# Residual, values' bias and convolution's bias added by accumulating DMAs from GpSimd's queue instead of GpSimd additions, in a graph attention and convolution kernel

## The chip, the cores and the metric

One core of one Trainium2 chip. The metric is the device time in microseconds; lower is better. The program has five engines with queues of their own: TensorE (PE in the profile, its weight loads PEld), VectorE (DVE), ScalarE (ACT), GpSimd (POOL) and SyncE (SP), which here only issues DMAs. Sixteen DMA engines move data for all queues.

## The reference, cut to what matters

There are 32 items of 512 rows and 512 columns and one 512x512 adjacency matrix of zeros and ones. Each item goes through an attention layer (8 heads of 64) and a graph convolution, each with a residual and a layer norm. All is float32.

```python
q = (x @ Wq + bq).reshape(b, n, H, HD)          # k and v likewise
scores = jnp.einsum('bihd,bjhd->bhij', q, k) / jnp.sqrt(jnp.float32(HD))
scores = scores + jnp.where(adj == 0, -1e9, 0.0)
weights = jax.nn.softmax(scores, axis=-1)
att = jnp.einsum('bhij,bjhd->bihd', weights, v)
x = _layernorm(x + att)
norm_adj = adj * deg_inv_sqrt[:, None] * deg_inv_sqrt[None, :]
out = jnp.einsum('nm,bmo->bno', norm_adj, x @ weight) + bias
x = _layernorm(x + out)
```

Three additions in it are touched here: `x + att`, the bias `bv` of the values, and the convolution's `bias`.

## The kernel before, in words

The main path is `unshifted`, lines 50 to 961. A second program, `general`, runs only if a count of unfit numbers is above zero. The 32 items are taken in turn by the loop at line 843. An item `b` has two halves. Each half is a **stretch** of attention for two of the four groups of two heads (line 514: `sc`, the scores, then `av`, the products with the values), followed by a stretch of other matrix products. After the first stretch come the keys and queries of item `b + 1` (14 steps of `main`). After the second come the convolution of item `b - 1` (`conv["first"]`, then `conv["second"]`) and the values of item `b + 1`. Keys, values and convolution use seven products of sub-matrices instead of eight, and the values use the scheme twice.

The order is written out by hand. `play` (line 106) runs the steps of `main` and after step `n` what the table `beside` holds for `n`. Operations on TensorE, VectorE, ScalarE and GpSimd are issued through `InOrder`, so each engine's queue keeps program order, and the profile shows all of them at line 45. The DMAs on SP are not pinned; the framework sets their order and all semaphore waits. The tiles that matter:

- `YT[b]` (profile: `yT`), 128 partitions x 4 blocks of 512 columns, 1 MiB, two buffers: the attention's result, then the normed rows. VectorE transposes the product into `yb` and four DMAs scatter it into `YT` (line 509). `scale` (608) divides by the sums, on VectorE, in the item's own second half. `add` (615) adds the residual, on GpSimd, after step 0 of the *next* item's first half. Then `measure` (633), `root`, `norm` (643, ScalarE) and `low` (661, VectorE) follow in that half. `lift` (666) adds the convolution's bias, on GpSimd, after step 11. `grow` (670, ScalarE) scales `YT` in the second half, and the last additions of `convolve` read it.
- `R[b]` (profile: `xr`), 1 MiB: the rows of `x` for the residual, loaded by `load_residual` (184) with four SP DMAs of 256 KB, at line 848 near the start of the item after. It shares its space with `zT` of the convolution.
- `V[b]` (profile: `v`), 1 MiB, one buffer: the values. ScalarE puts and VectorE adds the products into it, and one GpSimd addition (`spread_last`, 401) lies between. `bias_values` (420) adds `bv_r`, a row copied to all 128 partitions, in four GpSimd additions. They are queued after step 17 of the second half, behind `combined` (the four subtractions `combine`, 165, on the turned `x` of item `b + 2`) and ahead of the accumulation of the exponentials (`acc`, line 466) of the next stretch.
- `wqv` (profile: `wqv`), 1792 KB of weights: it holds the queries' weights or the values' weights in turn. `swap` (259) fetches the other set with one SP DMA, for the values at the start of the second stretch, for the queries after step 17.

The attention's two loops and the table of the steady state's second half:

```python
for g in gs:
    scores(b, g)
for g in gs:
    accumulate(b, g)
...
beside = {
    1: parts[:1] + fold0, 3: parts[1:], 5: fold1, 6: grow[:1], 7: end["inverse"], 8: grow[1:2],
    9: grow[2:3] + scale[:1], 10: grow[3:] + scale[1:2], 11: scale[2:3], 13: turn0, 14: scale[3:],
    15: turn1 + combined[:2], 17: combined[2:] + back_to_queries + bias_v,
}
```

Of the kernel before, what the change touches and what calls it, by code (L numbers as in the profile page):

```python
# [15 lines left out]
ALU = mybir.AluOpType  # L16
AX = mybir.AxisListType

P = 128
# [31 lines left out]
def unshifted(  # L51
# [15 lines left out]
    B, N, D = x.shape  # L67
    NT = N // P
# [4 lines left out]
    LAST = B - 1  # L73
    tensor, vector, scalar, gpsimd = (InOrder(tc, e) for e in (nc.tensor, nc.vector, nc.scalar, nc.gpsimd))
# [17 lines left out]
    def bank(shape, name="mm"):  # L92
        psum["n"] += 1
        return psum["pool"].tile(shape, F32, name=name, tag=f"bank{-psum['n'] % 8}", bufs=1)
# [89 lines left out]
    def load_residual(b):  # L184
        if b < LAST - 1:
            t = acts.tile([P, NT, D], F32, name="xr", tag="zT", bufs=1)
        else:
            t = wk[:, 3:].rearrange("p k u o -> p k (u o)")
        R[b] = [t[:, i, :] for i in range(NT)]
        for i in range(NT):  # L190
            nc.sync.dma_start(R[b][i], x[b, ts(i, P), :])
# [174 lines left out]
    KQ, V = {}, {}  # L366
# [5 lines left out]
    def values_of(b):  # L372
# [44 lines left out]
        leaf = seven(LEAF, multiply_quarters, put_quarters, add_quarters, (4, P))  # L417
        return leaf + [spread_last] + seven(OUTER, multiply, put, add)

    def bias_values(b, n, engine=gpsimd):  # L420
        engine.tensor_add(V[b][:, n, :], V[b][:, n, :], bv_r)

# [27 lines left out]
    E, ACC, AV, SM, YT, HI, LO = {}, {}, {}, {}, {}, {}, {}  # L450
# [87 lines left out]
    def sums(b, c, p):  # L538
        for q in range(4):
            parts = ACC[b, ORDER[2 * c + q // 2]]  # L540
            for k, a in enumerate(parts):
                tensor.matmul(
                    p[32 * q : 32 * (q + 1), :], sel[:, c, :], a[:, q % 2, :],
                    start=k == 0, stop=k == len(parts) - 1,
                )
        if c == 0:
            SM[b] = wqv[:, 6].rearrange("p u n -> p (u n)")
            vector.tensor_scalar(SM[b], p, 1e-36, None, op0=ALU.max)
        else:
            vector.scalar_tensor_tensor(SM[b], p, 1e-36, SM[b], op0=ALU.max, op1=ALU.add)  # L550
# [23 lines left out]
    def finish(b):  # L574
# [16 lines left out]
        def inverse(c, p):  # L591
            sT = SM[b]
            p = p.rearrange("p (i a k r) -> p i a k r", i=NT, a=2, k=2)
            for i in range(NT):
                tensor.transpose(p[:, i].rearrange("p a k r -> p (a k r)"), sT[:, ts(i, P)], ident)
            if c == 0:
                t["inv"] = small.tile([P, NT, H], F32, name="inv")
            inv = t["inv"].rearrange("p i (a c k) -> p i a c k", a=2, c=2)
            vector.reciprocal(inv[:, :, :, c], p[:, :, :, :, c])
# [70 lines left out]
        def grow(i):  # L670
            x1 = YT[b][:, i, :]
            scalar.activation(x1, x1, AF.Copy, scale=rdeg[:, i : i + 1])

        all_, behind = range(NT), (NT - 1, *range(NT - 1))
        return dict(
            sums0=[lambda: sums(b, 0, bank([P, N]))], inverse0=[lambda: inverse(0, bank([P, N]))],
            sums1=[lambda: sums(b, 1, bank([P, N]))], inverse1=[lambda: inverse(1, bank([P, N]))],
            turn_values=[lambda: turn_values(ORDER[-1], bank([P, N]))],
# [5 lines left out]
            lift=each(lift, *((3, 0, 1, 2) if b == LAST else behind)),  # L684
            grow=each(grow, *(all_ if b == LAST else behind)),
# [128 lines left out]
    v = values_of(0)  # L814
# [28 lines left out]
    for b in range(B):  # L843
        one, two = ORDER[:2], ORDER[2:]
        f[b], c[b] = finish(b), convolve(b)
        ahead, back = f.get(b - 1), c.get(b - 2)
        if 1 < b < LAST:
            load_residual(b - 1)
        if b + 2 < B:
            load_x(b + 2, 0)  # L850
        if b == LAST:
            load_residual(b)
        stretch(b, one, back["measure"][:3] if back else ())

        def folds(gs):
            return [[lambda g=g, b=b: fold(b, g)] for g in gs]

        def turns(b=b + 2):
            if b >= B:
                return [], [], []  # L860
            return [lambda: turn(b, 0)], [lambda: turn(b, 1)], [lambda k=k: combine(b, k) for k in range(4)]

        fold0, fold1 = folds(one) if b < LAST else ([], [])
        rest = back["measure"][3:] + back["root"] if back else []
        store = back["store"] if back else []
        if b < LAST:
            k0, k1 = keys_and_queries(b + 1, 0), keys_and_queries(b + 1, 1)
            main = [p for pair in zip(k0, k1) for p in pair]
            if b == 0:
                exact = each(compare, *range(NT))  # L870
                weights = each(lambda k: weigh_part(w1, gpsimd, k), *range(4))
                beside = {
                    1: fold0, 2: [degrees], 3: weights[:1], 4: fold1, 5: weights[1:2] + exact[:1], 6: exact[1:2],
                    7: weights[2:3], 8: exact[2:3], 9: weights[3:], 10: exact[3:],
                }
            else:
                measure, norm, low = ahead["measure"], ahead["norm"], ahead["low"]
                scale = ahead["inverse"] + ahead["scale"] if b == 1 else []
                beside = {
                    0: rest + scale + ahead["add"], 1: store[:1] + fold0, 2: store[1:2], 3: store[2:3] + fold1,  # L880
                    4: store[3:] + measure[:2], 5: measure[2:] + ahead["root"] + [quarters], 7: norm[:1] + ahead["judge"],
                    8: norm[1:2] + low[:1], 9: norm[2:3] + low[1:2], 10: norm[3:] + low[2:3],
                    11: low[3:] + ahead["lift"],
                }
            play(main, beside)
        else:
            e = f[b]
            conv = c[b - 1]
            play(conv["first"], {
                0: rest + store[:1] + conv["parts"][:0], 1: store[1:2] + ahead["judge"] + conv["parts"][:1],  # L890
                2: store[2:] + e["sums0"],
                3: conv["parts"][1:] + e["inverse0"] + ahead["grow"],
            })

        if b < LAST:
            swap(1)
        stretch(b, two, f[b]["pairs"][0] + f[b]["pairs"][1] if b == LAST else ())

        fold0, fold1 = folds(two) if b < LAST else ([], [])
        turn0, turn1, combined = turns()  # L900
        if b + 2 < B:
            load_x(b + 2, 1)
        if b < LAST:
            end = f[b]
            v, bias_v = values_of(b + 1), each(bias_values, *((b + 1, n) for n in range(NT)))
            back_to_queries = [lambda: swap(0)] if b < LAST - 1 else []
            if b == 0:
                play(v, {
                    1: fold0, 5: fold1, 8: turn0, 9: turn1 + combined[:2], 10: bias_v + combined[2:] + back_to_queries,
                })  # L910
            else:
                conv = c[b - 1]
                second = conv["second"]
                k = 6 if b < LAST - 1 else 8
                main = conv["first"] + v[:k] + second[:1] + v[k:9] + second[1:2] + v[9:10] + second[2:3] + v[10:] + second[3:]
                grow, parts, scale = ahead["grow"], conv["parts"], end["scale"]
                if b < LAST - 1:
                    beside = {
                        1: parts[:1] + fold0, 3: parts[1:], 5: fold1, 6: grow[:1], 7: end["inverse"], 8: grow[1:2],
                        9: grow[2:3] + scale[:1], 10: grow[3:] + scale[1:2], 11: scale[2:3], 13: turn0, 14: scale[3:],  # L920
                        15: turn1 + combined[:2], 17: combined[2:] + back_to_queries + bias_v,
                    }
                else:
                    measure, norm, low = end["measure"], end["norm"], end["low"]
                    beside = {
                        0: [lambda: load_residual(LAST - 1)], 1: parts[:1] + fold0, 3: parts[1:], 5: fold1,
                        6: grow[:1], 7: end["inverse"], 8: grow[1:2] + scale[3:], 9: grow[2:3] + scale[:1], 10: grow[3:] + scale[1:3] + end["add"],
                        14: measure[:2], 15: measure[2:3], 16: measure[3:] + end["root"],
                        17: norm[:1] + bias_v, 18: norm[1:2] + low[:1], 19: norm[2:3] + low[1:2],
                        20: norm[3:] + low[2:3], 21: low[3:] + end["lift"],  # L930
                    }
                play(main, beside)
# [6 lines left out]
    end, held, e = f[LAST], c[LAST - 1], c[LAST]  # L939
# [17 lines left out]
    p = bank([1, 1])  # L957
# [287 lines left out]
```

## Time and profile before

| | |
|---|---|
| median of 3 runs | 2732.55 us (2730.91 to 2732.78) |
| the profiled execution, its own time | 2731.85 us |
| its span | 2730.0 us |
| TensorE's clock | 0.998 |
| busy: TensorE, VectorE, ScalarE, GpSimd | 2700.8, 2023.7, 1260.5, 2026.7 us |
| GpSimd: `acc` (374 additions of 128x1024) | 886.6 us |
| GpSimd: `v` + `bv_r`, `yT` + `b_r`, `yT` + `xr` | 160.6, 156.9, 149.2 us |
| DMA moved | 256.75 MB, mean 94 GB/s |
| `xr` loads on SP | 116 of 256 KB in the loop, median 3.5 us to landing |
| `wqv` swaps on SP | 61 of 1792 KB, median 7.6 and 7.0 us to landing |

A row of the timeline or of the groups names engine, line and operation, then the tile written, an arrow, and the tiles read. Times are from the start of the span. A value in square brackets is the idle time ahead of a row and what ended it. The chain of waits is followed back from the last instruction, at each step to what released it. In the windows, "DMA share" is the mean busy share of the sixteen DMA engines.

### The profile page before, as it was taken

Reading aid. Unit: us, or ns where it says so; the run is one execution under the profiler, and the core shown is the slowest. Engines: PE = TensorE matmul, PEld = TensorE weight load, DVE = VectorE, ACT = ScalarE, POOL = GpSimd, SP = SyncE. Lnnn points to the kernel's source line nnn. Section 1 sums busy time; section 2 is a strip of 40 time slices with the busy share of each in tenths; the row PEclk is TensorE's granted clock in tenths of the full one; section 3 lists DMA queues with packets and bytes.
Section 4 is the critical chain, followed back from the end, with each engine's and each line's share of the span. In section 5 each row is a group of like instructions: output and inputs, shape, how many; then the busy total and the mean of one; then the engine's idle time right before and its main releaser. Section 6 shows DMA issues by size and latency. Waiting matters only on the chain.

```text
span 2730.0 us, 36290 instructions
## 1 busy us (share of the span) xinstructions
PE 2700.8 (99%) x13284; PEld 1907.7 (70%) x13284; DVE 2023.7 (74%) x2809; ACT 1260.5 (46%) x1807; POOL 2026.7 (74%) x1335
## 2 busy tenths in 40 slices
PE   9999999999999999999999999999999999999997
PEld 6676676766767767767667677677676676766765
DVE  4777776777777778767777777777777776777777
ACT  3335444454444454444544445444445444454444
POOL 5778777778777787777777777877778777778775
PEclk9999999999999999999999999999999999999999
DMA  6222333323333233333232332333333333323321
GB/s 181 86 74 88 101 89 99 107 69 105 93 105 97 76 103 104 89 97 97 82 104 86 103 106 73 101 107 90 94 90 92 101 89 98 107 70 104 98 61 45
DMA packets 388186, 256.75 MB, mean 94 GB/s; under 512 B 278816, under 2 KB 346400, under 8 KB 379936
## 3 DMA queue, kind: packets, MB, share of 16 engines
q1 hardware_dynamic: 386848, 252.78, 30.8%
q8 instruction: 107, 1.75, 0.3%
q10 hardware_dynamic: 1152, 1.57, 0.2%
q14 instruction: 79, 0.65, 0.1%
HBM read 183.77 MB, written 37.22 MB: 81 GB/s over the span
## 4 chain that ended last, share of the span: by engine, by line
PE 97%; DVE 2%; ACT 0%; DMA 0%; issue 0%; POOL 0%; SPq 0%; POOLq 0%; DVEq 0%; ACTq 0%
PE mm L45 64%; PE sc L45 17%; PE av L45 16%; DVE st L45 0%; DVE yT L45 0%; DVE xT L45 0%; DVE lo L45 0%; DVE v L45 0%; DVE kq L45 0%; POOL y L45 0%; DMA xr<-in_x_dram 0%; SPq L509 0%; DVE e L45 0%; DVE mv L45 0%; DVE folded L45 0%
## 5 line engine op out<-in xcount | busy, mean ns | idle before, releaser
L45 ACT ACTIVATE e<-e 128x1024 f32<-128x1024 f32 x512 | 541.3, 1057 | 598.1 <-DVE e L45 565.2
L45 DVE SCALAR_TENSOR_TENSOR e<-sc,maskT 128x1024 f32<-128x1024 f32 x512 | 584.9, 1214 | 99.4 <-PE sc L45 99.4
L45 POOL TENSOR_TENSOR acc<-acc,e 128x1024 f32<-128x1024 f32 x248 | 589.1, 2376 | 19.5
L45 POOL TENSOR_TENSOR xT<-xT 128x512 f32<-128x512 f32 x250 | 342.8, 1385 | 176.4 <-DVE xT L45 168.9
L45 PE MATMUL mm<-xT,wk 128*128 128x256 f32 x1792 | 463.4, 381 | 2.3 <-DVE kq L45 2.3
L45 PE MATMUL mm<-xT,wqv 128*128 128x256 f32 x1792 | 459.9, 379 | 0.0
L45 PE MATMUL sc<-kq 64*128 64x512 f32 x2048 | 458.7, 596 | 0.2 <-DVE kq L45 0.2
L45 PE MATMUL av<-e,v 128*64 128x512 f32 x2048 | 453.6, 595 | 0.3
L45 POOL TENSOR_TENSOR acc<-e 128x1024 f32<-128x1024 f32 x126 | 297.5, 2362 | 133.7 <-ACT e L45 133.7
L45 PEld LDWEIGHTS mm<-xT,wk 128*128 128x128 f32 x1792 | 337.4, 190 | 72.7 <-DVE mv L45 23.5
L45 PEld LDWEIGHTS mm<-xT,wqv 128*128 128x128 f32 x1792 | 340.5, 190 | 46.3
L45 PEld LDWEIGHTS av<-e,v 128*64 128x64 f32 x2048 | 146.5, 137 | 300.1 <-issue 242.1
L45 PEld LDWEIGHTS sc<-kq 64*128 64x128 f32 x2048 | 191.7, 186 | 235.3 <-issue 181.6
L45 ACT ACTIVATE kq<-mm,bias 128x256 f32<-128x256 f32 x512 | 214.5, 473 | 288.2 <-PE mm L45 285.5
L45 PE MATMUL mm<-wqv,xT 128*128 128x128 f32 x1736 | 302.2, 320 | 4.5 <-DVE v L45 4.5
L45 PEld LDWEIGHTS mm<-wqv,xT 128*128 128x128 f32 x1736 | 261.6, 191 | 27.8 <-issue 3.9
L45 DVE STREAM_TRANSPOSE yb<-av 128x512 f32<-128x512 f32 x127 | 91.0, 717 | 253.3 <-DMA yT<-yb 197.6
L45 DVE TENSOR_TENSOR v<-v,mm 128x512 f32<-128x512 f32 x221 | 146.2, 685 | 149.9 <-PE mm L45 148.9
L45 PE MATMUL mm<-w,zT 128*128 128x256 f32 x992 | 229.7, 379 | 0.2 <-DVE xT L45 0.2
L45 POOL TENSOR_TENSOR yT<-yT,b_r 128x512 f32<-128x512 f32 x126 | 156.9, 1277 | 64.3 <-DVE lo L45 64.3
L45 PEld LDWEIGHTS mm<-w,zT 128*128 128x128 f32 x992 | 186.0, 190 | 25.3 <-issue 1.4
L45 PE MATMUL mm<-adjT,hi 128*128 128x512 f32 x512 | 201.6, 397 | 0.7 <-ACT e L45 0.7
(133 smaller groups left out, 3465.1 us busy)
## 6 DMA issues: line engine op xcount, KB each, us to landing
wqv<-wv_parts SPq DMA_DIRECT2D x31, 1792.0 KB, 7.6
wqv<-wq_parts SPq DMA_DIRECT2D x30, 1792.0 KB, 7.0
yT<-yb SPq DMA_DIRECT2D x508, 64.0 KB, 2.4
out_dram<-y SPq DMA_DIRECT2D x120, 256.0 KB, 2.0
xr<-in_x_dram SPq DMA_DIRECT2D x118, 256.0 KB, 3.4
x<-in_x_dram SPq DMA_DIRECT2D x124, 128.0 KB, 2.7
e<-in_x_dram SPq DMA_DIRECT2D x124, 128.0 KB, 2.6
wk<-in_x_dram SPq DMA_DIRECT2D x8, 256.0 KB, 2.7
```

The source lines that it names most:

```text
L45: return self.tc.keep_in_program_order(op(*args, **kwargs))
```

## The change

Three sets of GpSimd additions become DMAs that add to what their destination holds, issued from GpSimd's queue, one of 1 MiB each:

- the residual of items 1 to 29: from `x` in DRAM straight into `YT[b]`, after `scale[3:]` at step 14 of the item's own second half. `load_residual` for these items is gone from SP's queue, and `add` for them from step 0 of the next item.
- the convolution's bias of items 0 to 29: the row `b1` in DRAM, read once per partition and block, into `YT`, where `lift` stood.
- the bias of the values of items 2 to 30: the row `bv` in DRAM, in the same way, into `V`, where `bias_v` stood.

Items 0 (residual), 0 and 1 (values), 30 and 31 keep the additions where these lists leave them out. The arithmetic of the reference is otherwise unchanged.

```diff
--- before.py
+++ after.py
@@ -417,6 +417,12 @@
         leaf = seven(LEAF, multiply_quarters, put_quarters, add_quarters, (4, P))
         return leaf + [spread_last] + seven(OUTER, multiply, put, add)
 
+    def gather(to, source):
+        gpsimd.dma_start(to, source, accum_op=ALU.add)
+
+    def rows(v):
+        return bass.AP(tensor=v.tensor, offset=v.offset, ap=[[0, P], [0, NT], [1, D]])
+
     def bias_values(b, n, engine=gpsimd):
         engine.tensor_add(V[b][:, n, :], V[b][:, n, :], bv_r)
 
@@ -672,7 +678,14 @@
             scalar.activation(x1, x1, AF.Copy, scale=rdeg[:, i : i + 1])
 
         all_, behind = range(NT), (NT - 1, *range(NT - 1))
+        def residual():
+            gather(YT[b], x[b].rearrange("(i p) o -> p i o", p=P))
+
+        def raise_all():
+            gather(YT[b], rows(b1))
+
         return dict(
+            residual=[residual], raise_all=[raise_all],
             sums0=[lambda: sums(b, 0, bank([P, N]))], inverse0=[lambda: inverse(0, bank([P, N]))],
             sums1=[lambda: sums(b, 1, bank([P, N]))], inverse1=[lambda: inverse(1, bank([P, N]))],
             turn_values=[lambda: turn_values(ORDER[-1], bank([P, N]))],
@@ -844,8 +857,6 @@
         one, two = ORDER[:2], ORDER[2:]
         f[b], c[b] = finish(b), convolve(b)
         ahead, back = f.get(b - 1), c.get(b - 2)
-        if 1 < b < LAST:
-            load_residual(b - 1)
         if b + 2 < B:
             load_x(b + 2, 0)
         if b == LAST:
@@ -877,10 +888,10 @@
                 measure, norm, low = ahead["measure"], ahead["norm"], ahead["low"]
                 scale = ahead["inverse"] + ahead["scale"] if b == 1 else []
                 beside = {
-                    0: rest + scale + ahead["add"], 1: store[:1] + fold0, 2: store[1:2], 3: store[2:3] + fold1,
+                    0: rest + scale + (ahead["add"] if b == 1 else []), 1: store[:1] + fold0, 2: store[1:2], 3: store[2:3] + fold1,
                     4: store[3:] + measure[:2], 5: measure[2:] + ahead["root"] + [quarters], 7: norm[:1] + ahead["judge"],
                     8: norm[1:2] + low[:1], 9: norm[2:3] + low[1:2], 10: norm[3:] + low[2:3],
-                    11: low[3:] + ahead["lift"],
+                    11: low[3:] + ahead["raise_all"],
                 }
             play(main, beside)
         else:
@@ -917,8 +928,8 @@
                 if b < LAST - 1:
                     beside = {
                         1: parts[:1] + fold0, 3: parts[1:], 5: fold1, 6: grow[:1], 7: end["inverse"], 8: grow[1:2],
-                        9: grow[2:3] + scale[:1], 10: grow[3:] + scale[1:2], 11: scale[2:3], 13: turn0, 14: scale[3:],
-                        15: turn1 + combined[:2], 17: combined[2:] + back_to_queries + bias_v,
+                        9: grow[2:3] + scale[:1], 10: grow[3:] + scale[1:2], 11: scale[2:3], 13: turn0, 14: scale[3:] + end["residual"],
+                        15: turn1 + combined[:2], 17: combined[2:] + back_to_queries + [lambda: gather(V[b + 1], rows(bv))],
                     }
                 else:
                     measure, norm, low = end["measure"], end["norm"], end["low"]
```

## The prediction

> **What bounds the kernel now.** I read the page's busy shares and its chain of waits first, then one item of the steady state (item 16 into 17, 1290 to 1400 us) in the timeline of each engine, and last the DMA share in windows of 3 us.
>
> ```profile
> span 2730.0 us, 36290 instructions
> PE 2700.8 (99%) x13284; PEld 1907.7 (70%) x13284; DVE 2023.7 (74%) x2809; ACT 1260.5 (46%) x1807; POOL 2026.7 (74%) x1335
> ...
> PE 97%; DVE 2%; ACT 0%; DMA 0%; issue 0%; POOL 0%; SPq 0%; POOLq 0%; DVEq 0%; ACTq 0%
> ```
>
> TensorE is the chain for 97% of the span, GpSimd (POOL) for 0%. The chain in order of time, over one item, has no other engine in it:
>
> ```profile
> 1295.83 7.07 PE sc L45 x32
> 1302.90 7.02 PE av L45 x32
> 1309.92 24.37 PE mm L45 x112
> 1334.29 7.07 PE sc L45 x32
> 1341.36 7.02 PE av L45 x32
> 1348.38 31.23 PE mm L45 x170
> 1379.61 7.07 PE sc L45 x32
> 1386.67 7.02 PE av L45 x32
> ```
>
> Each row starts where the last one ends: 1379.61 - 1295.83 = 83.78 us per item, all matmul, at a granted clock of 0.998. Work that GpSimd gives up inside an item can't shorten this; the change can only add waits. So I look for each thing that TensorE will wait for, and how early it is ready now. The critical one is the values' bias. GpSimd, SP and TensorE around it:
>
> ```profile
> 1371.34 5.19 POOL L45 TENSOR_TENSOR xT<-xT 128x512 f32<-128x512 f32 x4 [5.04 <-DVE xT L45]
> 1376.50 4.95 POOL L45 TENSOR_TENSOR v<-v,bv_r 128x512 f32<-128x512 f32 x4
> 1384.24 2.37 POOL L45 TENSOR_TENSOR acc<-e 128x1024 f32<-128x1024 f32 x1 [2.79 <-ACT e L45]
> ...
> 1386.61 7.09 PE L45 MATMUL av<-e,v 128*64 128x512 f32 x32
> ...
> 1372.73 0.34 SPq L260 DMA_DIRECT2D wqv<-wq_parts  x1
> 1379.76 1.77 SPq L191 DMA_DIRECT2D xr<-in_x_dram  x4
> ```
>
> The reader is to see that the biased values are ready at 1376.50 + 4.95 = 1381.45, and first used at 1386.61: 5.2 us to spare. The bias cannot start before 1376.50, since the four subtractions ahead of it on GpSimd wait for VectorE's turning of x. So a replacement has 10.1 us, from 1376.50 to 1386.61. The DMA engines are not idle then (columns: busy us of PE, PEld, DVE, ACT, POOL, clock, DMA share, GB/s):
>
> ```profile
> 1370.00:1373.00 3.00, 3.00 (x16) 2.64 (x15) 2.03 (x4) 0.00 (x0) 1.58 (x2) 1.00 0.28 81
> 1373.00:1376.00 3.00, 3.00 (x16) 2.64 (x15) 1.71 (x3) 0.00 (x0) 2.92 (x3) 1.00 0.77 216
> 1376.00:1379.00 3.00, 3.00 (x15) 2.65 (x14) 1.37 (x2) 0.00 (x0) 3.00 (x4) 1.00 0.93 397
> 1379.00:1382.00 3.00, 3.00 (x15) 1.46 (x15) 1.97 (x3) 0.03 (x1) 2.45 (x2) 1.00 0.40 104
> 1382.00:1385.00 3.00, 3.00 (x16) 1.36 (x14) 3.00 (x3) 2.85 (x3) 0.76 (x1) 1.00 0.68 250
> ```
>
> From 1373 to 1379 that is the weights' swap (1792 KB), after 1379 the residual's load (4 x 256 KB).
>
> **What the skill says.** "DMA: Bandwidth & Descriptors", section on SWDGE, HWDGE and iDMA: an accumulating DMA must be issued from GpSimd, whose own cores write the descriptors, and all queues end on the same 16 DMA engines. The section on the anatomy of one DMA prices a copy on that path at 2.0 us plus bytes over 436 GB/s. No DMA is issued from GpSimd in the trace of before, so it neither agrees nor disagrees. "Collectives: The Full Stack", Part 3: a reducing transfer reads two sources per chunk, the old value too, and ran at half the rate of a copy (measured 1.93 times). Again the trace has none. "TensorE: Matmul & The Clock Gate", Part 1: an idle window of about 3.4 us can halve TensorE's clock for about as long again. No gap here is long enough to show it.
>
> **The change part by part.** Sums are made against the profiled execution, 2731.85 us (span 2730.0 and 1.85 around it), 0.7 below the median of 2732.55. Counts: 29 residuals (items 1 to 29), 29 values' biases (V of items 2 to 30), 30 convolution biases (items 0 to 29), one DMA of 1 MiB each.
>
> *Removed:* per item 4 additions each of the residual (1276 ns), of the values' bias (1288 ns) and of the convolution's (1277 ns): 5.1 us each, 15.4 us of GpSimd per item. None is on the chain, so 0 us. VectorE stalls less beside GpSimd (the lo rows take 0.74 to 1.17 us); also off the chain, 0. The 116 loads of xr leave SP's queue and 3.26 us of full DMA time per item (0.40 x 3 + 0.68 x 3). Behind them on SP stand the stores of yb at 1391.09, which wait for VectorE anyway: 0.
>
> *Residual, now at the end of the item's own second half.* It waits for the last scaling by 1/sum, which VectorE ends at 1368.24 + 0.68 = 1368.92, and stands on GpSimd ahead of the subtractions, which begin at 1371.34. GpSimd's time to issue isn't in the trace: between 0 and the 4.95 us of the additions it replaces. I take 1 us, which the 2.4 us of idle time cover. Above that it delays the subtractions and the values' bias behind them one for one, at most 2.6 us. The statistics that read its result start at 1403.52 (VectorE, yT), over 30 us later: 0.
>
> *Convolution's bias.* It waits for the last lo (VectorE, until 1332.39) as the additions did. Behind it on GpSimd is acc at 1338.92, which waits for ScalarE: covered. It shares the DMA engines with the other swap, issued at 1334.32 (4.9 us of full DMA time) and needed by the values' matmuls at 1355.70; its own result is first read at 1358.17 (ScalarE's yT by rdeg). Even at 11.4 us of DMA work from 1333.4 both land by 1346. Only if these engines were some 10 us slower would this wait show: 0.
>
> *Values' bias.* Here lies the cost. Full DMA time of one accumulating MiB: a plain MiB took 3.26 us (xr); read twice, 6.5 us. Lower bound 3.26 (if reading the old value hides). Upper bound: the only other read of one repeated 2 KB row is the load of bv_r, 256 KB, landed 6.3 us after issue; four times that is 25 us. I take 6.5. The engines' work from 1370.0, when the residual's transfer begins, until the values' bias is done: rest of the x load 0.28 x 3 = 0.84; swap (0.77 + 0.93) x 3 + 0.04 = 5.14; residual 6.5; values' bias 6.5; sum 18.98, so 1388.98. Full use is fair since the two GpSimd DMAs follow one another in their queue and the swap runs beside them. One us from the last byte to the semaphore (estimate from xr: shortest landing 2.6 us for 0.8 us of work, less 0.8 to begin) gives 1390.0, against 1386.61: TensorE stops 3.4 us. Behind the wait, in order, stand all its matmuls, and TensorE has no idle time to catch up in. 29 x 3.4 = 98.6 us.
>
> Sum: 2731.85 + 98.6 = 2830.5, call it **2830 us**. I add nothing for a throttled clock: 3.4 us is at its edge. If it triggers, up to 1.7 us per item, 49 us.
>
> **Rivals.**
>
> *B. The transfer is hidden: not slower, 2732 us.* One mechanism: the accumulate costs the DMA engines less than a doubled read. The stop vanishes where 1370 + 0.84 + 5.14 + 2G + 1 = 1386.6, so G = 4.8 us per MiB; at the lower bound of 3.26 it lands at 1383.5, 3.1 us early. For it: 3.26 us includes the ramp of four separate loads, and the swap reaches 397 GB/s, at which a doubled MiB takes 5.3. Against: that is still above 4.8. TensorE then keeps its 83.78 us per item. It can't gain more than the few us of its gaps, as the chain shows.
>
> *C. The accumulate is much slower than two reads.* Either the engines wait on each read-modify-write, or 512 reads of one 2 KB row of bv crowd one place in memory. At 12 us per MiB: 1370 + 5.98 + 24 + 1 = 1401, a stop of 14 us, 29 x 14 = 406 us, 3138. At the 25 us bound for the values alone, begun at 1377.5: 1403.5, a stop of 17 us, 3225. A mild case, 9 us per MiB: 8.4 us, 244 us, 2975. For it: nothing in this trace shows such an operation. Against: b_r, 256 KB of the same kind, landed 11.2 us after issue, but behind 2 MB of queued loads.
>
> *D. GpSimd's issue is the long part.* With 5 us per issue, the values' bias is issued at 1379.1 and written out by 1384.1. With the 6.5 us overlapped or not, it lands between 1388 and 1391.6: 1 to 5 us, 2770 to 2877. It looks like my forecast from outside; the GpSimd rows tell them apart.
>
> **How the numbers follow.** Forecast (stop of 0.2 to 6 us per item, D within it): 0.53. B, no stop: 0.22, of which 0.02 is a gain from something unseen. C (over 6 us, above 2906): 0.25, about half of it above 3000. About 0.2% (5.5 us) is what a measurement of this kernel can tell from no change. Faster 0.02, same 0.20, slower 0.78. The range runs from 2729 (B) to 3000, leaving out 0.12 of C above and the 0.02 below. The forecast's own range is 2738 to 2906.
>
> **What would show it.** Right: a wait of TensorE (av) for a DMA into v, 29 times, some 3.4 us; items of 87 us; windows of DMA share near 1.0 from the residual's start until av. yT must not be waited for by the statistics or by ScalarE. GpSimd rows of DMA issue near 1 us; more of it points to D. Wrong: items of 83.8 us with av starting as sc ends (B), a wait over 6 us or a stretch of full DMA share with low GB/s (C), or a clock below 0.99 with the same wait (the gate). The step I trust least is 6.5 us per accumulating MiB.

## The result, and the profile after

| | before | after |
|---|---|---|
| median | 2732.28 us (4 runs) | 2801.44 us (4 runs, 2796.81 to 2804.62) |
| ratio of after to before | | 1.0253, 95% interval 1.0235 to 1.027 |
| the profiled execution, and its span | 2731.85, 2730.0 us | 2801.22, 2799.4 us |
| TensorE's clock | 0.998 | 0.994 |

The change costs 69 us, 2.5%. The lines of the page of after that answer to those of before: span, busy shares, the queue of GpSimd's DMAs (packets, MB, share of 16 engines' span), the group of the products with the values (busy us and mean ns; then idle before it and what ended it), and the new issues with their median time to landing.

```profile
span 2799.4 us, 36062 instructions
PE 2714.9 (97%) x13284; PEld 1923.3 (69%) x13284; DVE 1993.1 (71%) x2809; ACT 1266.8 (45%) x1807; POOL 1681.0 (60%) x1071
...
q0 software_dynamic: 46464, 92.28, 19.9%
...
L45 PE MATMUL av<-e,v 128*64 128x512 f32 x2048 | 465.4, 608 | 55.8 <-DMA v<-in_L_gnn_bv_dram 49.1
...
yT<-in_L_gnn_bias_dram POOLq DMA_DIRECT2D x30, 1024.0 KB, 14.4
...
yT<-in_x_dram POOLq DMA_DIRECT2D x29, 1024.0 KB, 13.6
v<-in_L_gnn_bv_dram POOLq DMA_DIRECT2D x29, 1024.0 KB, 12.0
```

GpSimd gave up 346 us of busy time, and nothing came of it. TensorE now stands idle for 55.8 us ahead of `av`, nearly all of it until the DMA into `v` lands. It is also busy for 14.1 us more (2714.9 against 2700.8) with the same instructions. 55.8 + 14.1 = 69.9, against 69.4 between the spans: these two terms are the whole loss. (The chain of this profile breaks off after a few per cent of the span, so it isn't used.)

One item in the timelines of GpSimd and TensorE:

```profile
1318.54 1.30 POOL L45 DMA_DIRECT2D yT<-in_x_dram  x1 [2.93 <-DVE yT L45]
1320.68 5.19 POOL L45 TENSOR_TENSOR xT<-xT 128x512 f32<-128x512 f32 x4 [0.84 <-DVE xT L45]
1325.82 1.29 POOL L45 DMA_DIRECT2D v<-in_L_gnn_bv_dram  x1
...
1328.87 7.14 PE L45 MATMUL sc<-kq 64*128 64x512 f32 x32
1338.65 7.09 PE L45 MATMUL av<-e,v 128*64 128x512 f32 x32 [2.65 <-DMA v<-in_L_gnn_bv_dram]
```

The scores end at 1336.0 and `av` starts at 1338.65. Before, it started as the scores ended. The DMA engines in the same item (last two columns: share and GB/s):

```profile
1319.00:1322.00 3.00, 3.00 (x16) 2.64 (x15) 2.10 (x3) 0.00 (x0) 2.10 (x2) 1.00 0.81 153
1322.00:1325.00 3.00, 3.00 (x16) 2.64 (x15) 1.97 (x3) 0.00 (x0) 2.90 (x3) 1.00 1.05 176
1325.00:1328.00 3.00, 3.00 (x16) 2.64 (x15) 1.38 (x2) 0.00 (x0) 2.10 (x2) 1.00 1.12 343
1328.00:1331.00 3.00, 3.00 (x15) 1.56 (x15) 1.64 (x2) 0.00 (x0) 0.00 (x0) 1.00 1.04 380
1331.00:1334.00 3.00, 3.00 (x16) 1.35 (x14) 3.00 (x4) 2.55 (x3) 0.42 (x1) 1.00 1.04 210
1334.00:1337.00 3.00, 2.00 (x10) 0.58 (x6) 3.00 (x4) 2.78 (x4) 2.92 (x2) 1.00 0.92 168
```

Residual, swap and values' bias keep the engines full from 1322 to 1337. Where an accumulating DMA runs without the swap (the last row), full engines move less than half of the 380 GB/s they move where the swap runs.

Most of the second term is the clock. After some of the stops TensorE's next matmuls are slow, as its timeline shows for the item after:

```profile
1425.33 8.78 PE L45 MATMUL av<-e,v 128*64 128x512 f32 x32 [2.83 <-DMA v<-in_L_gnn_bv_dram]
```

In the windows of that stretch the column ahead of the DMA share is the granted clock:

```profile
1425.00:1428.00 3.00, 2.67 (x10) 1.17 (x12) 0.68 (x1) 1.69 (x2) 3.00 (x2) 0.74 0.00 0
1428.00:1431.00 3.00, 3.00 (x12) 1.04 (x10) 0.28 (x1) 0.00 (x0) 2.92 (x2) 0.69 0.00 0
```

The same 32 matmuls take 8.78 us here and 7.09 above. The `av` group is 465.4 - 453.6 = 11.8 us longer than before, seven such items of 1.69 us. The other 2.3 us of busy time come with the stops and not with the clock: in the last experiment below, with stops but a clock of 0.998 and `av` at 453.6 us, TensorE is busy 2703.0 us, also 2.2 us more than before.

### The profile page after: what moved, and what is told of

Same layout as the page of the kernel before. It is cut to its first block, busy times and chain, and to the rows that moved or that the text cites. A ratio compares the mean times of both kernels' runs of the same rounds, so it can differ in the third digit from the quotient of the medians.

```text
span 2799.4 us, 36062 instructions
## 1 busy us (share of the span) xinstructions
PE 2714.9 (97%) x13284; PEld 1923.3 (69%) x13284; DVE 1993.1 (71%) x2809; ACT 1266.8 (45%) x1807; POOL 1681.0 (60%) x1071
## 3 DMA queue, kind: packets, MB, share of 16 engines
q0 software_dynamic: 46464, 92.28, 19.9%
## 5 line engine op out<-in xcount | busy, mean ns | idle before, releaser
L45 PE MATMUL av<-e,v 128*64 128x512 f32 x2048 | 465.4, 608 | 55.8 <-DMA v<-in_L_gnn_bv_dram 49.1
L45 PEld LDWEIGHTS av<-e,v 128*64 128x64 f32 x2048 | 161.9, 139 | 354.0 <-issue 235.7
L45 POOL TENSOR_TENSOR xT<-xT 128x512 f32<-128x512 f32 x250 | 318.6, 1289 | 52.7 <-DVE xT L45 45.2
L45 POOL TENSOR_TENSOR rstd<-ve,minus_half 128x4 f32<-128x4 f32 (+1 forms) x66 | 66.0, 1000 | 267.1 <-DVE nmu L45 266.4
## 6 DMA issues: line engine op xcount, KB each, us to landing
wqv<-wq_parts SPq DMA_DIRECT2D x30, 1792.0 KB, 10.4
yT<-in_x_dram POOLq DMA_DIRECT2D x29, 1024.0 KB, 13.6
```

The costliest lines, as they stand in the source:

```text
L45: return self.tc.keep_in_program_order(op(*args, **kwargs))
```

## The experiments

My theory: TensorE waits for the values' bias and for nothing else of the change, because that transfer stands behind the residual's and shares the engines with the swap. The rivals: the other two DMAs cost by themselves; a DMA from GpSimd takes about 12 us whatever stands ahead; one row read 512 times is slow. All edits are made to the changed kernel.

**The values' bias back to additions.**

```diff
- 17: combined[2:] + back_to_queries + [lambda: gather(V[b + 1], rows(bv))],
+ 17: combined[2:] + back_to_queries + bias_v,
```

> The values' bias goes back to four GpSimd additions; the residual and the convolution's bias stay accumulating DMAs. My theory (the whole loss is TensorE waiting for the values' bias): no wait for v, 2732 us within 5. Rival (the other two DMAs cost by themselves, through the swaps or the stores of yb that share the DMA engines): above 2745 us.

Measured: 2732.15 us, ratio to before 1.0001 (0.9993 to 1.0009), clock 0.998; no wait of TensorE for `v`:

```profile
L45 PE MATMUL av<-e,v 128*64 128x512 f32 x2048 | 453.6, 595 | 0.3
```

The other 59 DMAs by themselves are free. They slow the swaps (median landing 12.1 and 10.4 us against 7.6 and 7.0 before), but TensorE doesn't wait for those. The loss is there only when the values' bias is a DMA too. What delays that DMA is the next question.

**The residual behind the values' bias.**

```diff
- 14: scale[3:] + end["residual"],
+ 14: scale[3:],
- 17: combined[2:] + back_to_queries + [lambda: gather(V[b + 1], rows(bv))],
+ 17: combined[2:] + back_to_queries + [lambda: gather(V[b + 1], rows(bv))] + end["residual"],
```

> The residual's DMA is issued from GpSimd after the values' bias instead of ahead of the subtractions. My theory (the values' bias stands in GpSimd's queue behind the residual's 6.3 us of transfer): it lands about 8 us after its issue instead of 12.0, TensorE doesn't stop, 2732 us within 5. Rival (a DMA from GpSimd takes some 12 us from issue to landing whatever is ahead of it): the stop stays near 2 us, 2795 to 2805 us.

Measured: 2780.67 us, ratio 1.0176 (1.0162 to 1.019). The page's group of `av` and the issue row:

```profile
L45 PE MATMUL av<-e,v 128*64 128x512 f32 x2048 | 455.3, 597 | 46.9 <-DMA v<-in_L_gnn_bv_dram 42.5
...
v<-in_L_gnn_bv_dram POOLq DMA_DIRECT2D x29, 1024.0 KB, 11.6
```

My number failed. Putting the residual behind gained 0.4 us of landing, not 4; the rival's range was missed too. Either the transfer takes over 8 us by itself, or what follows in the queue slows it as well. Later runs take these apart.

**The values' bias issued earlier, still behind the residual.**

```diff
- 17: combined[2:] + back_to_queries + [lambda: gather(V[b + 1], rows(bv))],
+ 17: [lambda: gather(V[b + 1], rows(bv))] + combined[2:] + back_to_queries,
```

> The values' bias is issued ahead of the last two subtractions, 2.6 us earlier at most, still behind the residual. My theory (queue of transfers): it lands at the same moment as now, its time from issue to landing grows by what it is issued earlier, 2790 to 2803 us. Rival (fixed time from issue): the stop shrinks by 2 us or more, 2735 to 2750 us.

Measured: 2804.84 us, ratio 1.0266 (1.025 to 1.0282), median landing 14.2 us after issue. The time is 2 us above my range, and the rival is out. Issued some 2 us earlier, it lands when it did: here its end is set by the transfers ahead and beside it, not by its issue.

**The swap behind the values' bias.**

```diff
- 17: combined[2:] + back_to_queries + [lambda: gather(V[b + 1], rows(bv))],
+ 17: combined[2:] + [lambda: gather(V[b + 1], rows(bv))]
+     + ([lambda: gpsimd.dma_start(wqv, stored[0])] if back_to_queries else []),
```

> The swap to the queries' weights is issued from GpSimd's queue behind the values' bias, instead of from SP 3.7 us ahead of it. My theory (the swap's 5.1 us of transfer shares the engines ahead of the values): the values land about 5 us earlier and TensorE doesn't stop for them, 2732 to 2737 us; the weights land some 6 us later and just in time. Rival (queues don't slow each other): 2795 to 2805 us.

Measured: 2751.27 us, ratio 1.0071 (1.0056 to 1.0087).

```profile
L45 PE MATMUL av<-e,v 128*64 128x512 f32 x2048 | 453.6, 595 | 17.0 <-DMA v<-in_L_gnn_bv_dram 13.6
...
v<-in_L_gnn_bv_dram POOLq DMA_DIRECT2D x29, 1024.0 KB, 10.6
```

My number failed by 14 us: the values land 1.4 us earlier, not 5. Moving the swap gives back 50 of the 69 us. That isn't the swap's share of the loss, since leaving out the residual instead gives back 52 (last experiment): the loss of this size needs both ahead of the values. Without the swap the residual lands 9.5 us after issue (13.6 in the changed kernel), and the values follow sooner. A stop of 0.6 us per item stays. The swap now stands right behind the values' bias in the same queue, and still it lands after 10.6 us.

**The values' bias alone.** The residual's load and both other additions are as before the change.

```diff
+        if 1 < b < LAST:
+            load_residual(b - 1)
...
- 0: rest + scale + (ahead["add"] if b == 1 else []),
+ 0: rest + scale + ahead["add"],
- 11: low[3:] + ahead["raise_all"],
+ 11: low[3:] + ahead["lift"],
- 14: scale[3:] + end["residual"],
+ 14: scale[3:],
```

> Only the values' bias is a DMA; the residual is loaded from SP and added by GpSimd as before, and so is the convolution's bias. My theory: no 6.3 us of residual ahead, but the load of xr (3.26 us of transfer) now runs beside it on SP's queue from 1379.8 in the clock of before, so it lands between 1386.1 (xr gives way) and 1389.3 (equal shares), a stop of 0 to 2.7 us: 2732 to 2810, likeliest 2770. Rival (fixed time from issue): 2795 to 2805 us with 12 us to landing.

Measured: 2833.81 us, ratio 1.0371 (1.0355 to 1.0387), landing 12.6 us after issue. That is above my range and worse than all three together. The `xr` load comes in beside it on SP's queue and lands in 8.9 us (3.4 before). The stops, 73.2 us or 2.5 per item, are within my range, near what equal shares gave (2.7); the clock adds 28.7 us in `av`, which I had left out.

**Overwriting instead of adding.**

```diff
-        gpsimd.dma_start(to, source, accum_op=ALU.add)
+        gpsimd.dma_start(to, source)
```

> The three DMAs overwrite their destination instead of adding to it, so the attention's result, the convolution's first input and the values are replaced by what is read (residual, biases). Same bytes from memory, same number of rows. My theory (adding costs a second read): the GpSimd queue's share falls from 19.9% to about 10%, 3.3 us per MiB, the values land about 7 us after issue, no stop, 2732 us. Rival (the cost is in this queue and its 2 KB pieces, not in adding): the share stays near 20%, 2795 to 2805 us.

Measured: 2731.68 us, ratio 0.9997 (0.9989 to 1.0006).

```profile
q0 software_dynamic: 23936, 92.28, 14.7%
...
v<-in_L_gnn_bv_dram POOLq DMA_DIRECT2D x29, 1024.0 KB, 9.1
```

No stop. But 14.7% is neither 10% nor 20%: 4.56 us of engine time per MiB (0.147 x 2729.1 / 88) against 6.33 when adding (0.199 x 2799.4 / 88), a factor of 1.39, with 1.94 times the packets. So adding is decisive here, but it isn't two reads' worth of time. This engine time isn't a fixed price either: it is the time that packets took, and with the `xr` load beside it, in the values' bias alone, it is 7.1 us per MiB (0.073 x 2833.3 / 29). The bytes are the same 92.28 MB in both kernels, so GB/s does not count a read of the old value.

**Many rows instead of one.**

```diff
- gather(V[b + 1], rows(bv))
+ gather(V[b + 1], x[b].rearrange("(i p) o -> p i o", p=P))
```

> The DMA into the values adds 512 different rows of 2 KB (the item's x) instead of the one row of bv 512 times, so the values are wrong by x. My theory (the double read sets the cost): no change, 2795 to 2805 us. Rival (many reads of one row crowd one place in memory): the DMA lands earlier than 12.0 us after issue, the stop shrinks, below 2775 us.

Measured: 2804.83 us, ratio 1.0265 (1.0249 to 1.0281), landing 12.1 us. For an adding DMA, reading one row 512 times costs nothing extra; this part of rival C is out.

**TensorE kept busy through the stop.**

```diff
         banks("products")
+        if gs == ORDER[:2] and 1 < b < LAST:
+            p = bank([P, N])
+            for _ in range(2):
+                tensor.matmul(p, ident, KQ[b, gs[0]][:, 0, :], start=True, stop=True)
```

> Two extra matmuls whose result is not used (128x512, together about 1.7 us) run on TensorE between the scores and the products of each first stretch of items 2 to 30, where it waits for v. My theory (of the 69 us lost, 14 are matmuls at a throttled clock after the longest stops): no stop is long enough to throttle, the clock is back at 0.998 and TensorE's other rows at their length, 2783 to 2793 us. Rival (the clock's fall has another cause): clock still 0.994, 2798 to 2806 us.

Measured: 2796.01 us, ratio 1.0232 (1.0218 to 1.0246), clock 0.998.

```profile
L45 PE MATMUL av<-e,v 128*64 128x512 f32 x2048 | 453.6, 595 | 9.2 <-DMA v<-in_L_gnn_bv_dram 5.9 <-ACT e L45 2.7
```

`av` is back at 453.6 us: the slow matmuls came from the idle stops. The time missed my range by 3 us; the two matmuls (57.5 us busy in all) take 57.5 / 29 = 1.98 us, not 1.7, and outlast the shorter stops.

**The values' bias first.** GpSimd's order is values, two subtractions, swap, residual.

```diff
- 14: scale[3:] + end["residual"],
+ 14: scale[3:],
- 17: combined[2:] + back_to_queries + [lambda: gather(V[b + 1], rows(bv))],
+ 17: [lambda: gather(V[b + 1], rows(bv))] + combined[2:]
+     + ([lambda: gpsimd.dma_start(wqv, stored[0])] if back_to_queries else []) + end["residual"],
```

> All three DMAs stay, in another order on GpSimd: the values' bias ahead of the last two subtractions, then the swap to the queries' weights (from GpSimd), then the residual. My theory as the runs so far leave it (about 10.5 us from issue to landing with nothing ahead, of which 2 us before the first byte): issued at 1374.1 in the clock of before, it lands near 1384.6, 2 us ahead of its use; no stop, 2732 us within 5. Rival (what follows in the same queue slows it too): a stop of 0.5 us or more per item, above 2745 us.

Measured: 2732.24 us, ratio 1.0 (0.9992 to 1.0008). The timelines of GpSimd and TensorE:

```profile
1291.05 1.29 POOL L45 DMA_DIRECT2D v<-in_L_gnn_bv_dram  x1 [0.35 <-DVE v L45]
...
1303.34 7.09 PE L45 MATMUL av<-e,v 128*64 128x512 f32 x32
```

And the windows of the transfer, with DMA share and GB/s last:

```profile
1291.00:1293.00 2.00, 2.00 (x11) 1.77 (x10) 0.77 (x2) 0.00 (x0) 1.95 (x2) 1.00 0.00 0
1293.00:1296.00 3.00, 3.00 (x16) 2.60 (x14) 1.30 (x2) 0.00 (x0) 2.92 (x4) 1.00 0.87 152
1296.00:1299.00 3.00, 3.00 (x16) 1.32 (x16) 2.24 (x3) 0.30 (x1) 0.88 (x1) 1.00 0.94 147
```

This is the transfer with nothing ahead of it; the swap and the residual are issued 3.9 and 4.5 us behind it. The DMA engines stand still for 2 us after the issue, then move about 150 GB/s at a share near 0.9, and it lands 10.7 us (median) after issue: near 1301.7, with `av` at 1303.34. With 12.3 us of lead all three DMAs are free, and GpSimd is busy 1727.4 us instead of 2026.7. It is no faster than before, since TensorE bounds both.

**Half the values' bias by DMA.**

```diff
- [lambda: gather(V[b + 1], rows(bv))]
+ [lambda: gather(V[b + 1][:, :2, :], rows(bv)[:, :2, :])] + bias_v[2:]
```

> Half of the values' bias (two of four blocks, 512 KB) by DMA, the other half by two GpSimd additions behind it; residual and swap as in the changed kernel. My theory (the DMA's own bytes take 6 to 7 us per MiB of engine time): it lands some 3 us earlier, about 9 us after issue, no stop, 2732 to 2737 us. Rival (the landing is set by what stands ahead and by fixed times): it lands over 11 us after issue, above 2770 us.

Measured: 2733.15 us, ratio 1.0005 (0.9996 to 1.0013), landing 9.5 us after issue, 0.9 us of stops in all. Half the bytes land 2.5 us sooner: the size counts, but less than 3.2 us per half MiB.

**The residual left out.**

```diff
- 14: scale[3:] + end["residual"],
+ 14: scale[3:],
```

> The residual of items 1 to 29 is left out altogether, so the layer norm works on the attention alone; the swap from SP and the other two DMAs as in the changed kernel. It tells what follows from what stands ahead: if the residual issued right behind the values' bias slows it (it landed 11.6 us after issue there), it lands now near 10.5 us, a stop of some 0.4 us, 2740 to 2750 us. If only what is ahead counts (the swap's last 2 us): 11.6 us again, 2775 to 2783 us.

Measured: 2749.04 us, ratio 1.0064 (1.0049 to 1.0079).

```profile
v<-in_L_gnn_bv_dram POOLq DMA_DIRECT2D x29, 1024.0 KB, 10.5
```

The swap from SP is ahead of it here, and it lands as early as with nothing ahead. So the 1.1 us more when the residual is issued right behind (11.6) come from the DMA that *follows* in the queue. This doesn't hold for every follower: the swap, a copy, right behind the values' bias left it at 10.6 us. No run shows whether that is because the swap doesn't add, or because in that run no swap ran ahead.

## Why the prediction was right, and which terms were off

The mechanism holds. **TensorE as the bound:** confirmed; two kernels that relieve GpSimd by 214 us (additions for the values) and by 299 us (values first) run at 1.0001 and 1.0 of before. **Residual and convolution's bias at nothing:** confirmed by the first experiment. **GpSimd's issue of 1 us:** it takes 1.30, within the idle time that I named; rival D falls. **The values' bias late, TensorE stopped 29 times:** confirmed; the stops (55.8 us), the slow matmuls behind some of them (11.8) and 2.3 us more of busy time make up the difference. **VectorE stalling less without these additions:** not so, as the last section shows; it was rightly put at 0, since it is off the chain.

The sizes were off, partly against each other. I had 98.6 us of stops, 3.4 per item; measured are 55.8, or 1.9. The transfer lands 12.0 us after its issue, where my sum gave 1390.0 - 1376.5 = 13.5. The engine time per accumulating MiB was nearly right, 6.33 for 6.5, but by luck: it isn't a plain MiB taken twice (rows from this queue cost 4.56, and adding 1.39 times that). Full use was right on average: the six rows of windows above sum to 17.9 us of engine time (3 us times each share) in 18 us, though single rows go up to 1.12. That is 1 us less work than my 18.98, and the values' bias of this item landed 12.8 us after its issue, within a spread of 11.2 to 13.0. No run splits the rest.

Against that I put the clock at nothing, with 49 us at most; it took 11.8, in seven items of 1.69 us where I had up to 1.7 for each. So 43 us too much for the stops and 14 too little for the rest: 2830 against 2801. That the errors partly cancel is luck too. (The 3.26 us of `xr` is 3.24 by the sum shown; it changes nothing.)

How the 12.0 us come about, from the runs: 10.7 with nothing ahead (values first), 10.5 with only the swap ahead (residual left out), 10.6 with only the residual ahead (swap behind), and 12.0 with both, where the swap has delayed the residual. So neither alone adds to the landing, and the two together add 1.5 us. The lead of 10.1 us is short of even the 10.5. It was not a fixed 10.1, though: I took the place behind all four subtractions as given, and values first, ahead of two of them, has 12.3. **Rival B** falls by its own term, 6.33 us per MiB where it needed 4.8. **Rival C** is refuted for the row that is read again and again. Its other half, that the engines wait on each read-modify-write, isn't settled: 150 GB/s at a share near 0.9 would fit it, but a read of the old value isn't in that figure.

On the clock, "TensorE: Matmul & The Clock Gate" (Part 1) has an idle window of about 3.4 us. Here the measurement decides: stops of 2.1 to 2.9 us slowed the matmuls behind them, in seven items, while others of up to 2.65 us didn't. On the reducing transfer, "Collectives: The Full Stack" (Part 3) has half a copy's rate; in this queue adding took 1.39 times the engine time of overwriting, so less than twice.

What stays open is why the share of accumulating DMAs goes with so few GB/s, in the engine or at the memory, and what fills the 2 us before the first bytes; no run here separates that.

## What to carry to other kernels

An addition moved from GpSimd into a DMA still takes 1.3 us of GpSimd for the issue here, and it turns the moment of the result from "issue plus the length of the addition" (5 us here) into "issue plus some 10.5 us for 1 MiB, plus what the transfers ahead, beside and behind add" (up to 3.7 us here, in the run issued earlier). Before such a move, take the lead from the earliest issue to the first use from the timeline, and order the queue by who is needed first: the same three DMAs cost 2.5% in one order and nothing in another, with the swap moved behind the values too. Where one engine is on the chain for 97% of the span, relieving another can gain next to nothing, and no run here was faster than before beyond its interval.

## What the runs showed of the hardware that was not expected

- From the issue of an accumulating DMA on GpSimd to its first bytes pass 2 us, in which the share is 0.00 (values first); GpSimd itself is done after 1.29.
- A DMA that follows in the same queue can delay the one ahead: 11.6 us to landing with the adding residual right behind it, 10.5 without. With the copying swap right behind it, it was 10.6.
- VectorE's small `ve<-mv,eps` rows (128x4) took 1.31 us on average before and 0.18 in the changed kernel. In one item of before such a row began at 1397.09 and ended at 1398.72, as GpSimd's addition of exponentials ended (1393.93 + 4.78 = 1398.71). The additions taken off GpSimd aren't the reason: with all three gone (overwriting) the rows took 1.3 us, and with two of the three kept (values alone) 0.16. In the changed kernel the row comes after the end of that addition: in one item the addition ended at 1348.00 and the row began at 1349.18. This was worth nothing off the chain.
